# Moving zero writes, layer norms and hidden units in the first two layers of an eight-stage network kernel

## The chip, the cores and the metric

The kernel runs on one core of a Trainium2 chip. A core has TensorE (PE in the profile; PEld is its weight load), VectorE (DVE), ScalarE (ACT), GpSimd (POOL) and SyncE (SP, which here only issues DMAs). TensorE writes its results to PSUM, from where VectorE and ScalarE fetch them into SBUF. The metric is the device time of one execution in microseconds; lower is better.

## The reference

Sixteen blocks of 128 tokens with 256 channels (`x`, float32) go through four pairs of a cross attention and a feed-forward layer. Each of the eight layers begins with a layer norm of `x` over the channels and adds its output to `x`. The change is in the first pair:

```python
def _layernorm(x, axis=-1, eps=1e-05):
    m = jnp.mean(x, axis=axis, keepdims=True)
    v = jnp.var(x, axis=axis, keepdims=True)
    return (x - m) / jnp.sqrt(v + eps)

# first attention: 32 heads of 8 channels, keys and values from ctx (128 tokens a block)
q = apply_axial_rope((x @ Wq).reshape(b, n, 32, 8), pos)
k, v = jnp.split(ctx @ Wkv, 2, axis=-1)          # k gets the same rotation
w = softmax(einsum('bqhd,bkhd->bhqk', q, k) / sqrt(8))
out = einsum('bhqk,bkhd->bqhd', w, v).reshape(b, n, 256) @ Wout + bout

# product-key layer: 4 heads, two sets of 128 keys, 2048 hidden units, 8 of them chosen a head
sim1, sim2 = q1 @ keys[:, :, 0], q2 @ keys[:, :, 1]
s1, i1 = top_k(sim1, 8); s2, i2 = top_k(sim2, 8)
final_scores, pk_idx = top_k(s1[..., :, None] + s2[..., None, :], 8)
hidden = silu(x . e_down[chosen]) * relu(final_scores)
out = sum over chosen of hidden * e_up[chosen]

x = x + attention(_layernorm(x)); x = x + product_key(_layernorm(x)); ...
```

## The kernel before

One program holds all layers; `run` (from L1625 on) loads the packed weights of each layer into two alternating SBUF slots, "even" and "odd", and calls the layers in order. The program is traced through a layer that makes all semaphores and, for each engine, a fixed order of instructions: a planner goes through the traced instructions with a model of their costs and lets each engine take, whenever it is free in that model, the earliest traced instruction that is ready. On the chip every engine then runs its instructions strictly in that order. `tc.issue_after(ins)` puts what is traced inside it, as far as it is on the engine of `ins`, behind `ins`. `tc.high_priority()` lets a few matmuls go ahead. Tiles of one tag in a pool share the pool's buffers in turn.

**Start.** `setup` (L69 on) loads two blocks of `x`, small constants and makes the identity. `run` then loads the attention's weights, the other blocks of `x`, and the product-key layer's weights `w_f0` (5 MB) into the odd slot; it writes zeros into a tile `zero` (L1652) and sends it 14 times to a scratch in DRAM (for a later layer). `rope_tables` (L185 on) makes cosines and sines on VectorE and ScalarE from `pos`.

**A norm.** `ln` (L136 on) makes for each block two VectorE instructions, BATCH_NORM_STATS2 (L143) and BATCH_NORM_AGGREGATE (L144), then for the group two on GpSimd, an addition (L119) and a power (L120, `rsqrt_pool`), and then for each block one VectorE instruction, xn (L154). `lnT` transposes the result on TensorE (pxT, L168) and fetches it to xnT by ScalarE and VectorE in turn (L67, L65).

**First attention** (`l0_attn`). It first writes zeros into three tiles `vx` (values with zeros between the heads, 1280 columns each) and `own` (zeros with ones, for the sums of the softmax): these are GpSimd's MEMSETs of L234 and L235. `inputs(g)` makes a group's norms: group 0 is blocks 0 and 1, then four blocks a group. For one block, `front` makes queries, keys and values (pqk, pv; L251 to L267), `turn` the transposes and the block-diagonal keys `kbd` (L279, L282 on GpSimd), and `start(b, c)` a half of the heads: `l0_terms` makes the scores S on TensorE (L322, into a single PSUM buffer), and twice, for half of S, a maximum (L330), a subtraction into E (L331, the second one is kept as `l0_last`) and the exponential on ScalarE (L332). `l0_heads` transposes E (pT, L181), copies (eT, L344), multiplies with `vx` and `own` into po (L350), and divides (rz L361, oT L362). `l0_out` projects (py, L370) and adds to `x` (L371). The loop over blocks runs them interleaved: the second half of block b is started while the first half is finished, and `front` is two blocks ahead. In it, group b // 4 + 2 is traced at b = 3, 7, 11, ahead of everything else of that block, and group 1 before the loop, tied behind `l0_last`.

**Product-key layer** (`l0_ffn`). Its pools take over the SBUF and PSUM of the attention's. `normed(g)` makes the norm of two blocks. `scores(b)` makes the queries fq (L403) and, in `peer_scores`, their products with both sets of keys (fs, L462; sim, L466), maxima and thresholds on VectorE and GpSimd. `units(b, q)` makes a quarter of the 16 groups of hidden units (fh, L417) and their SiLU (sh, L421). `peer_table(b, half)` makes, for a half of the keys, a table of sums g of each of four heads (two heads on GpSimd, L501, two on ScalarE, L507) and keeps what is over the threshold (L511, VectorE). `peer_weights` transposes the tables into one sum (r, L525) and multiplies with the units (wT, L529). `peer_up` multiplies with the last matrix (fy, L538). Before the loop come norm, scores, table and four units of block 0, and two units of block 1 (`first`); in the loop each half makes the next table behind the current wT, and the next block's units two by two, if they were not made.

Of the kernel before, what the change touches and what calls it, by code (L numbers as in the profile page):

```python
# [8 lines left out]
F32 = mybir.dt.float32  # L9
# [6 lines left out]
ALU = mybir.AluOpType  # L16
# [4 lines left out]
P = 128  # L21
# [31 lines left out]
class Net:  # L53
# [50 lines left out]
        at, w = ROWS[name]  # L104
        return self.rows[:, at : at + w]

    def load(self, pool, name, tag, step=2048):

        src = self.a[name]
        n = src.shape[1]  # L110
        t = pool.tile([P, n], F32, tag=tag, name=f"w_{name}")
        for i, at in enumerate(range(0, n, step)):
            end = min(n, at + step)
            self.nc.sync.dma_start(out=t[:, at:end], in_=src[:, at:end])
        return t

    def rsqrt_pool(self, out, var, n):

        self.nc.gpsimd.tensor_tensor(out, var, self.eps5.to_broadcast([P, n]), ALU.add)  # L119
        self.nc.gpsimd.tensor_tensor(out, out, self.mhalf.to_broadcast([P, n]), ALU.pow)  # L120

    def rsqrt(self, pool, x, n, tag, key):

# [32 lines left out]
            )  # L156
        return xn

    def lnT(self, pool, psum, bs, ptag="tr", rsqrt=None, bufs=None):

        nc = self.nc
        xn = self.ln(pool, bs, rsqrt=rsqrt, bufs=bufs)
        n = len(bs)
        xT = pool.tile([P, 2, n * P], F32, tag="xnT", name=f"xnT{bs[0]}")
        for c in range(2):
            ps = psum.tile([P, 512], F32, tag=ptag, name=f"pxT{bs[0]}_{c}")
            for i in range(n):
                nc.tensor.transpose(  # L168
                    ps[:, i * P : (i + 1) * P], xn[:, i, c * P : (c + 1) * P], self.ident
                )  # L170
            self.evac(xT[:, c, :], ps[:, : n * P])
        return xn, xT
# [42 lines left out]
    def l0_attn(self, w):  # L215

        nc, tc = self.nc, self.tc
        Wq = w[:, 0:512].rearrange("p (c n) -> p c n", c=2)
        Wk = w[:, 512:768]
        Wv = w[:, 768:1024]  # L220
        Wo = w[:, 1024:1536].rearrange("p (c n) -> p c n", c=2)
        with ExitStack() as es:
            op = es.enter_context(tc.tile_pool(name="l0o", bufs=1))
            xp = es.enter_context(tc.tile_pool(name="l0x", bufs=2))
            sp = es.enter_context(tc.tile_pool(name="l0s", bufs=2))
            kp = es.enter_context(tc.tile_pool(name="l0k", bufs=3))
            tr = es.enter_context(tc.tile_pool(name="l0tr", bufs=3, space=PSUM))
            sc = es.enter_context(tc.tile_pool(name="l0sc", bufs=1, space=PSUM))
            pvp = es.enter_context(tc.tile_pool(name="l0pv", bufs=1, space=PSUM))

            own = op.tile([P, 160], F32, tag="own", name="own")
            vx = [op.tile([P, 8, 160], F32, tag=f"vx{k}", name=f"vx{k}") for k in range(3)]
            for t in (*vx, own):
                nc.gpsimd.memset(t, 0.0)  # L234
            nc.gpsimd.memset(own.rearrange("p (i k) -> p i k", k=40)[:, :, 0:8], 1.0)  # L235
            xTs, turned, ready, terms, outs, after = {}, {}, {}, {}, {}, {}

            def inputs(g):
                bs = [b for b in range(max(4 * g - 2, 0), 4 * g + 2) if b < self.nb]
                if bs:  # L240
                    xT = self.lnT(xp, tr, bs, rsqrt=self.rsqrt_pool)[1]
                    for i, b in enumerate(bs):
                        xTs[b] = xT[:, :, i * P : (i + 1) * P]

            def front(b):

                if b >= self.nb:
                    return
                xT = xTs.pop(b)
                pqk = tr.tile([P, 2, 256], F32, tag="tr", name=f"pqk{b}")  # L250
                nc.tensor.matmul(pqk[:, 1, :], self.ctxT[:, b, :], Wk, start=True, stop=True)  # L251
                for c in range(2):
                    nc.tensor.matmul(pqk[:, 0, :], xT[:, c, :], Wq[:, c, :], start=c == 0, stop=c == 1)
                pv = tr.tile([P, 32, 8], F32, tag="tr", name=f"pv{b}")
                nc.tensor.matmul(pv.rearrange("p h d -> p (h d)"), self.ctxT[:, b, :], Wv, start=True, stop=True)
                qk = sp.tile([P, 512], F32, tag="qk", name=f"qk{b}")
                t = sp.tile([P, 512], F32, tag="t", name=f"t{b}")
                by_head = lambda a: a.rearrange("p (h a two) -> p h a two", a=4, two=2)
                src = pqk.rearrange("p t (h a two) -> p (t h) a two", a=4, two=2)
                nc.vector.tensor_tensor(by_head(qk), src, bc(self.cosT[:, b], 1, 64), ALU.mult)  # L260
                for k in range(2):
                    nc.vector.tensor_tensor(
                        by_head(t)[:, :, :, k], src[:, :, :, 1 - k], bc(self.sinT[:, b, :, k], 1, 64), ALU.mult
                    )
                nc.gpsimd.tensor_tensor(qk, qk, t, ALU.add)
                v = vx[b % 3]
                nc.scalar.copy(  # L267
                    v.rearrange("p g (i k) -> p g i k", k=40)[:, :, :, 0:8], pv.rearrange("p (g i) d -> p g i d", i=4)
                )
                turned[b] = (qk, v)  # L270

            def turn(b):

                if b >= self.nb:
                    return
                qk, v = turned.pop(b)
                ps = self.transposes(tr, lambda i: qk[:, i * P : (i + 1) * P], 4, f"pqkT{b}")
                qkT = kp.tile([P, 4, P], F32, tag="qkT", name=f"qkT{b}")
                nc.scalar.copy(qkT, ps)  # L279
                kbd = kp.tile([P, 2, 4, P], F32, tag="kbd", name=f"kbd{b}")  # L280
                for c in range(2):
                    after[b] = nc.gpsimd.tensor_tensor(  # L282
                        kbd[:, c], bc(qkT[:, 2 + c, :], 1, 4), bc(self.mask8, 2, P), ALU.mult
                    )
                ready[b] = (qkT, kbd, v)

            def start(b, c):
                if b < self.nb:
                    terms[b, c] = self.l0_terms(sp, kp, sc, b, c, *ready[b][:2])

            inputs(0)
            front(0)
            front(1)
            turn(0)
            turn(1)
            start(0, 0)
            with tc.issue_after(self.l0_last.ins):
                inputs(1)
            for b in range(self.nb):
                if b % 4 == 3:  # L300
                    inputs(b // 4 + 2)
                start(b, 1)
                front(b + 2)
                outs[b] = sp.tile([P, 2, P], F32, tag="oT", name=f"oT{b}")
                self.l0_heads(sp, kp, tr, pvp, b, 0, terms.pop((b, 0)), ready[b][2], own, outs[b])
                if b:
                    self.l0_out(tr, b - 1, outs.pop(b - 1), Wo, after[min(b + 1, self.nb - 1)])
                start(b + 1, 0)
                self.l0_heads(sp, kp, tr, pvp, b, 1, terms.pop((b, 1)), ready.pop(b)[2], own, outs[b])
                turn(b + 2)  # L310
            b = self.nb - 1
            self.l0_out(tr, b, outs.pop(b), Wo, after[b])
# [61 lines left out]
    def l0_ffn(self, w):  # L374

        nc, tc = self.nc, self.tc
# [4 lines left out]
        with ExitStack() as es:  # L381
            xp = es.enter_context(tc.tile_pool(name="f0x", bufs=2))
# [3 lines left out]
            mm = es.enter_context(tc.tile_pool(name="f0mm", bufs=4, space=PSUM))  # L386
# [4 lines left out]
            def normed(g):  # L391
                if g * 2 < self.nb:
                    bs = list(range(2 * g, min(2 * g + 2, self.nb)))
                    _, xT = self.lnT(xp, mm, bs, ptag="mm", rsqrt=self.rsqrt_pool)
                    for i, b in enumerate(bs):
                        xTs[b] = xT[:, :, i * P : (i + 1) * P]

# [27 lines left out]
            chosen = scores(0)  # L425
            G = self.peer_table(gp, 0, 0, chosen)
            sh = [units(0, q) for q in range(4)]
            first = [units(1, q) for q in range(2)] if self.nb > 1 else []
            for b in range(self.nb):
                more = b + 1 < self.nb  # L430
                nxt, after = first, None
                first = []
# [1192 lines left out]
    def run(self):  # L1625

        tc = self.tc
# [7 lines left out]
        loaded = []  # L1635
        pools = [None, self.wpool]
        for i, (_, _, stages) in enumerate(plan):
            if i == 0:

                with tc.tile_pool(name="w0", bufs=1) as pool:  # L1640
                    loaded = [self.load(pool, *plan[0][:2], step=1024)]
                    load = lambda out, in_: self.nc.sync.dma_start(out=out, in_=in_)
# [3 lines left out]
                            load(self.rows, self.a["rows"][0:NALL].partition_broadcast(P))  # L1646
                        load(self.x[b], self.a["x"][b])
                    load(self.gains, self.a["gains"])
                    loaded.append(self.load(self.wpool, *plan[1][:2]))

                    zero = pool.tile([P, 8 * D], F32, tag="zero", name="zero")
                    self.nc.gpsimd.memset(zero, 0.0)  # L1652
# [161 lines left out]
```

## Time and profile before

| | |
|---|---|
| median of 3 runs | 2497.4 us (2489.95 to 2499.14) |
| profiled execution | 2492.25 us, its span 2490.5 us |
| mean granted TensorE clock | 0.974 |
| first attention, 0 to 281 us | PE busy 249.61, DVE 229.91, ACT 153.07, POOL 75.55 us |
| product-key layer, 281 to 695 us | PE 389.90, DVE 342.89, ACT 220.71, POOL 167.78 us |
| the other layers, 695 to 2490.5 us | PE 1642.30, DVE 1150.22, ACT 674.44, POOL 503.60 us |

A line of the timeline has the start of an instruction or of several alike in us, their time in us, the engine, the line in the kernel, the operation, the output and inputs by the program's names, the shapes and the count. In brackets is how long the engine had been idle and who ended that. Busy times are sums of the instructions' times; as matmuls overlap, a busy TensorE is not TensorE at its peak. The granted clock is a share of full speed.

### The profile page before, as it was taken

To read this page: it belongs to the slowest core of one execution; us is meant where nothing else is said; L and a number is where in the kernel's file an instruction comes from. 1 tells how busy PE (TensorE), PEld (TensorE's weight loads), DVE (VectorE), ACT (ScalarE), POOL (GpSimd) and SP (SyncE) were. 2 spreads that over 40 slices of the span, in tenths; PEclk is the share of its full clock that TensorE was granted. 3 is DMA by queue.
4 is the path that set the end of the run, shared out by engine and by line. 5 is a ranking of instruction groups with operands and counts; after the bars stand their busy time and mean duration, and the time that the engine had idled before them with its cause. 6 is when DMAs were issued, how large, how long until landed. Compare 5 with 4: busy or idle time off the path is not lost. (4 is left out here: it accounts for less than half of the span.)

```text
span 2490.5 us, 39604 instructions
## 1 busy us (share of the span) xinstructions
PE 2281.8 (92%) x14876; PEld 1709.7 (69%) x14876; DVE 1723.0 (69%) x3904; ACT 1048.2 (42%) x2778; POOL 746.9 (30%) x678
## 2 busy tenths in 40 slices
PE   6999799999989999998997778899899999999798
PEld 3666589898977777775884455555577777776465
DVE  6888788888865555565574999831466666668964
ACT  3656455455533443432331333411455555554121
POOL 3222234343411322222002433100222332224665
PEclk8999899999999999998999899999999999999999
DMA  9000200000030000002223000000100000000000
GB/s 376 17 2 2 86 1 1 1 1 1 1 121 2 19 10 10 10 13 84 69 71 137 25 14 10 1 0 1 69 1 1 1 1 1 1 1 1 7 13 15
DMA packets 29678, 74.57 MB, mean 30 GB/s; under 512 B 6688, under 2 KB 21160, under 8 KB 23856
## 3 DMA queue, kind: packets, MB, share of 16 engines
q1 hardware_dynamic: 25200, 62.06, 6.7%
q0 software_dynamic: 3072, 8.39, 1.0%
q8 instruction: 119, 1.95, 0.3%
q10 hardware_dynamic: 1216, 1.59, 0.2%
q14 instruction: 71, 0.58, 0.1%
HBM read 46.07 MB, written 25.95 MB: 29 GB/s over the span
## 5 line engine op out<-in xcount | busy, mean ns | idle before, releaser
L501 POOL TENSOR_TENSOR g<-sim 128x1024 f32<-128x1024 f32 x64 | 140.2, 2212 | 221.1 <-ACT sim L466 186.4
L181 PE MATMUL pT<-ident,E 128*128 128x128 f32 x1280 | 196.0, 283 | 9.8 <-POOL E L631 7.5
L511 DVE SCALAR_TENSOR_TENSOR g<-g,th 128x1024 f32<-128x1024 f32 x128 | 194.3, 1577 | 0.0
L181 PEld LDWEIGHTS pT<-ident,E 128*128 128x128 f32 x1280 | 147.0, 144 | 51.7 <-issue 21.8
L507 ACT ACTIVATE g<-sim 128x128 f32<-128x128 f32 x512 | 159.8, 390 | 32.0 <-PE r L525 31.5
L626 ACT ACTIVATE E<-E,mx 128x128 f32<-128x128 f32 x256 | 99.5, 390 | 160.1 <-DVE mx L623 138.7
L1464 POOL TENSOR_TENSOR E<-E,rs 128x512 f32<-128x512 f32 x64 | 66.6, 1041 | 302.0 <-DVE rs L1463 148.6
L1459 ACT ACTIVATE E<-S,mx,sc 128x128 f32<-128x128 f32 x256 | 113.9, 455 | 98.8 <-DVE mx L1455 89.6
L525 PE MATMUL r<-ident,g 128*128 128x128 f32 x1024 | 124.6, 277 | 19.9 <-DVE g L511 19.8
L525 PEld LDWEIGHTS r<-ident,g 128*128 128x128 f32 x1024 | 115.4, 142 | 27.7 <-DVE g L511 17.5
L661 PE MATMUL py<-w_w_l,oT 128*128 128x256 f32 x512 | 128.1, 383 | 5.2 <-DVE x L663 3.6
L1492 PE MATMUL py<-w_w_l,oT 128*128 128x256 f32 x512 | 131.1, 383 | 0.1
L1492 PEld LDWEIGHTS py<-w_w_l,oT 128*128 128x128 f32 x512 | 93.6, 190 | 46.9 <-issue 39.2
L631 POOL TENSOR_TENSOR E<-E,rs 128x512 f32<-128x512 f32 x64 | 66.7, 1042 | 193.5 <-DVE rs L630 119.8
L417 PE MATMUL fh<-xnT,w_w_f 128*128 128x128 f32 x1024 | 122.7, 279 | 0.0
L600 PE MATMUL pt<-xnT,w_w_l 128*128 128x256 f32 x512 | 121.1, 382 | 0.0
L661 PEld LDWEIGHTS py<-w_w_l,oT 128*128 128x128 f32 x512 | 93.9, 190 | 39.4 <-issue 20.1
L417 PEld LDWEIGHTS fh<-xnT,w_w_f 128*128 128x128 f32 x1024 | 118.6, 194 | 1.8
L538 PE MATMUL fy<-w_w_f,wT 128*128 128x256 f32 x512 | 118.4, 379 | 0.0
L1406 PE MATMUL pq<-xnT,w_w_l 128*128 128x256 f32 x512 | 116.2, 380 | 1.0 <-ACT xnT L67 0.6
L600 PEld LDWEIGHTS pt<-xnT,w_w_l 128*128 128x128 f32 x512 | 94.9, 192 | 15.2 <-issue 2.5
L1406 PEld LDWEIGHTS pq<-xnT,w_w_l 128*128 128x128 f32 x512 | 94.8, 190 | 14.4 <-ACT sqk L1372 1.2
(401 smaller groups left out, 5505.7 us busy)
## 6 DMA issues: line engine op xcount, KB each, us to landing
w_w_f<-in_w_f SPq DMA_DIRECT2D x14, 1024.0 KB, 11.2
sent<-zero SPq DMA_DIRECT2D x14, 1024.0 KB, 20.2
w_w_l<-in_w_l SPq DMA_DIRECT2D x14, 1024.0 KB, 11.1
xb<-sent SPq DMA_DIRECT2D x38, 128.0 KB, 2.0
back<-yb SPq DMA_DIRECT2D x38, 128.0 KB, 1.9
x<-in_x SPq DMA_DIRECT2D x16, 128.0 KB, 4.9
out<-x SPq DMA_DIRECT2D x16, 128.0 KB, 1.7
ctx<-in_ctx ACTq DMA_DIRECT2D x1, 1024.0 KB, 8.4
```

Source lines behind the costliest of these rows:

```text
L181: self.nc.tensor.transpose(ps[:, i, :], src(i), self.ident)
L417: nc.tensor.matmul(ps[:, k, :], down[:, c, a * P : (a + 1) * P], xT[:, c, :], start=c == 0, stop=c == 1)
L501: nc.gpsimd.tensor_tensor(g, bc(sim[:, 2 * h, 8 * half : 8 * half + 8], 2, P), bc(sim[:, 2 * h + 1, :], 1, 8), ALU.add)
L507: nc.scalar.activation(g[:, k, :], sim[:, 2 * h + 1, :], AF.Identity, bias=sim[:, 2 * h, a : a + 1])
L511: nc.vector.scalar_tensor_tensor(gf, gf, th[:, h : h + 1], gf, ALU.is_ge, ALU.mult)
L525: nc.tensor.matmul(ps[:, k, :], G[h][:, 4 * q + k, :], self.ident, start=h == 0, stop=h == 3, is_transpose=True)
L538: self.nc.tensor.matmul(py, wT[:, k, :], up[:, a, :], start=a == 0, stop=a == 15)
L600: nc.tensor.matmul(ps[:, k], A[:, h + k, c, :], xT[:, c, :], start=c == 0, stop=c == 1)
L661: nc.tensor.matmul(pys[b], oT[:, j, :], Wo[:, h, :], start=h == 0, stop=h == 15)
L1406: nc.tensor.matmul(ps[:, l], Wq[:, c, h * P : (h + 1) * P], xT[:, c, :], start=c == 0, stop=c == 1)
L1459: nc.scalar.activation(E[:, j, :], S[:, j, :], AF.Exp, bias=mx[:, j : j + 1], scale=sc[:, i, 0, r, j : j + 1], accum_out=rs[:, j : j + 1],)
L1492: nc.tensor.matmul(pys[b], oT[:, j, :], Wo[:, h, :], start=h == 0, stop=h == 15)
```

## The change

Four edits in the first two layers:

1. The zeros of `vx` and `own` are traced after `inputs(0)`, tied on GpSimd behind the power of that first norm (`self.root`).
2. In the attention's loop, `start(b, 1)` is traced first, and `inputs` of the later groups behind it, tied on VectorE behind the last subtraction of that `start`.
3. The product-key layer's norm of blocks 0 and 1 is made in the attention at b = 6, with the attention's pools, tied like the norms of edit 2. Its transposed result lies in 512 columns that are added to the tile of `w_f0` (`xT2`), and `normed(0)` takes it from there.
4. Before the loop of the product-key layer, four units of block 1 are traced instead of two. The loop then makes none for that block.

```diff
-    def load(self, pool, name, tag, step=2048):
+    def load(self, pool, name, tag, step=2048, more=0):
         src = self.a[name]
         n = src.shape[1]
-        t = pool.tile([P, n], F32, tag=tag, name=f"w_{name}")
+        t = pool.tile([P, n + more], F32, tag=tag, name=f"w_{name}")
...
-        self.nc.gpsimd.tensor_tensor(out, out, self.mhalf.to_broadcast([P, n]), ALU.pow)
+        self.root = self.nc.gpsimd.tensor_tensor(out, out, self.mhalf.to_broadcast([P, n]), ALU.pow)
...
-    def lnT(self, pool, psum, bs, ptag="tr", rsqrt=None, bufs=None):
+    def lnT(self, pool, psum, bs, ptag="tr", rsqrt=None, bufs=None, xT=None):
...
-        xT = pool.tile([P, 2, n * P], F32, tag="xnT", name=f"xnT{bs[0]}")
+        xT = pool.tile([P, 2, n * P], F32, tag="xnT", name=f"xnT{bs[0]}") if xT is None else xT[:, :, : n * P]
...
-            for t in (*vx, own):
-                nc.gpsimd.memset(t, 0.0)
-            nc.gpsimd.memset(own.rearrange("p (i k) -> p i k", k=40)[:, :, 0:8], 1.0)
...
             inputs(0)
+            with tc.issue_after(self.root.ins):
+                for t in (*vx, own):
+                    nc.gpsimd.memset(t, 0.0)
+                nc.gpsimd.memset(own.rearrange("p (i k) -> p i k", k=40)[:, :, 0:8], 1.0)
             front(0)
...
             for b in range(self.nb):
-                if b % 4 == 3:
-                    inputs(b // 4 + 2)
                 start(b, 1)
+                with tc.issue_after(self.l0_last.ins):
+                    if b % 4 == 3:
+                        inputs(b // 4 + 2)
+                    if b == min(6, self.nb - 1):
+
+                        bs = [k for k in range(2) if k < b]
+                        self.aheadT = bs, self.lnT(xp, tr, bs, rsqrt=self.rsqrt_pool, xT=self.xT2)[1]
                 front(b + 2)
...
-                    _, xT = self.lnT(xp, mm, bs, ptag="mm", rsqrt=self.rsqrt_pool)
+                    if bs == self.aheadT[0]:
+                        xT = self.aheadT[1]
+                    else:
+                        _, xT = self.lnT(xp, mm, bs, ptag="mm", rsqrt=self.rsqrt_pool)
...
-            first = [units(1, q) for q in range(2)] if self.nb > 1 else []
+            first = [units(1, q) for q in range(4)] if self.nb > 1 else []
...
-                    loaded.append(self.load(self.wpool, *plan[1][:2]))
+
+                    loaded.append(self.load(self.wpool, *plan[1][:2], more=512))
+                    self.xT2 = loaded[1][:, 10240:10752].rearrange("p (c n) -> p c n", c=2)
```

## The prediction

> **What bounds the kernel now.** I read the busy time by stages first, since the page's 92% for TensorE is a mean over seven very different layers. The change touches only 0 to about 340 us: the first attention (0 to 281 us) and the start of the product-key layer. The first fence is that table. After each stretch and its length come the busy times of PE, PEld, DVE, ACT and POOL (instructions in brackets), then the granted TensorE clock, the DMA share and GB/s.
>
> ```profile
> 20.00:30.00 10.00, 4.08 (x18) 1.87 (x17) 8.82 (x22) 4.09 (x5) 3.95 (x5) 0.65 1.00 383
> 30.00:40.00 10.00, 7.45 (x54) 4.94 (x52) 8.91 (x20) 3.90 (x8) 1.31 (x3) 0.84 1.02 428
> 40.00:50.00 10.00, 6.71 (x75) 4.44 (x73) 8.47 (x18) 4.91 (x9) 4.26 (x7) 0.84 1.01 422
> ...
> 200.00:240.00 40.00, 39.33 (x497) 25.19 (x491) 33.97 (x45) 23.62 (x37) 10.70 (x11) 1.00 0.01 2
> 280.00:320.00 40.00, 29.86 (x211) 27.16 (x212) 26.55 (x70) 18.34 (x49) 13.77 (x17) 0.83 0.33 132
> ```
>
> Three places leave TensorE idle: the first 10 us (it does 0.13 us of work), 20 to 50 us, where VectorE is 87% busy and TensorE 61% at a reduced clock, and 280 to 312 us. Between them the attention runs at 15.2 us a block: the POOL rows of kbd start at 69.33 and, 12 blocks later, at 252.00, and (252.00 - 69.33) / 12 = 15.2.
>
> The second view is the timeline of the start.
>
> ```profile
> 3.21 3.60 DVE L193 COPY ang<-pos 128x32 f32<-128x32 f32 x1 [3.21 <-DMA pos<-in_pos]
> 3.23 3.37 POOL L234 MEMSET vx<- 128x1280 f32 x3
> ...
> 3.39 3.44 DVE L143 BATCH_NORM_STATS2 st<-x 128x6 f32<-128x256 f32 x1
> ...
> 6.54 0.22 POOL L234 MEMSET own<- 128x160 f32 x1
> ...
> 8.56 0.76 POOL L120 TENSOR_TENSOR rs<-rs,mhalf 128x2 f32<-128x2 f32 x1
> ...
> 9.30 0.19 DVE L213 COPY sinT<-sFalse 128x64 f32<-128x64 f32 x1
> 9.40 0.73 DVE L154 TENSOR_SCALAR xn<-x,mv,rs 128x256 f32<-128x256 f32 x2
> ```
>
> A VectorE copy of 32 columns takes 3.60 us, where one of 64 takes 0.19: it ends at 6.81, just behind the last zero-writing (6.54 + 0.22 = 6.76). The copy is held while GpSimd writes zeros, and the first statistics wait behind it.
>
> The third view is the timeline from 29 us.
>
> ```profile
> 29.40 0.72 DVE L143 BATCH_NORM_STATS2 st<-x 128x6 f32<-128x256 f32 x2
> ...
> 31.99 1.38 DVE L154 TENSOR_SCALAR xn<-x,mv,rs 128x256 f32<-128x256 f32 x4 [1.09 <-POOL rs L120]
> ...
> 33.29 1.21 DVE L330 TENSOR_REDUCE mx<-S 128x8 f32<-128x1024 f32 x1
> ```
>
> The scores of block 0's second half were made by 24.75 + 2.09 = 26.84, yet their maximum starts at 33.29: statistics and norms of blocks that nobody needs yet stand in front of it.
>
> The fourth view is the passage between the layers.
>
> ```profile
> 280.13 0.70 PE L370 MATMUL py<-w_w_l,oT 128*128 128x256 f32 x2 [1.41 <-DVE oT L362]
> ...
> 285.63 3.76 PE L403 MATMUL fq<-xnT,w_w_f 128*128 128x128 f32 x16 [0.30 <-ACT xnT L67]
> ...
> 303.14 0.45 PE L525 MATMUL r<-ident,g 128*128 128x128 f32 x1 [4.52 <-DVE g L511]
> ...
> 305.99 5.51 PE L417 MATMUL fh<-xnT,w_w_f 128*128 128x128 f32 x32
> ...
> 311.34 3.00 PE L525 MATMUL r<-ident,g 128*128 128x128 f32 x26
> ```
>
> From the last projection (ends 280.83) to the first query matmul, 4.8 us pass with only the norm of blocks 0 and 1 in between, though those blocks were finished some 200 us earlier. Then fq takes 3.76 us at half clock; the same 16 matmuls take 1.95 at 314.18.
>
> **Zeros behind the first norm.** Without the hold, the first statistics end near 3.39 + 0.39 = 3.8 instead of 6.83: 3.05 us, and the path (statistics, POOL, xn, TensorE) has no other cover, so it counts in full. Against it stands the new place: the five zero-writings (3 x 1.12 + 0.22 + 0.12 = 3.7 us) start as pow ends, where VectorE's last table copies and xn run. Here a rule of the Trainium skill speaks against the change ("SBUF — State Buffer", section "Who interferes with whom"): GpSimd and a VectorE copy or tensor_scalar in a two-port mode exclude each other for a whole instruction, whichever comes first. By the rule with xn as such an instruction, xn would start near 6.2 + 3.7 = 9.9 instead of 9.40: 0.5 lost. The rows speak less strictly: xn takes 0.316 to 0.414 us in 32 instances, 256 columns at one a cycle of that page's 0.96 GHz (an estimate of 0.27), so it runs in no such mode; and the three table copies before 9.30 overlap pow unharmed. Only the last copy races with the first zero. I take 3.0 gained and keep -0.5. The zeros are needed by the copy into vx (13.80), 4 us later; POOL's next own work starts at 14.75.
>
> **Norms behind subtractions.** Statistics of blocks 6 to 15 leave the start: 10 x (0.31 + 0.08) = 3.9 us; and xn of blocks 6 to 13: 8 x 0.345 = 2.8. VectorE sets the pace there, so 6.7 us. They return at blocks 3, 7 and 11, behind the second subtraction of a half. VectorE's rows at 80 to 240 us show 16 waits of 16.3 us in all for S, about 1 us each; four statistics (1.56) nearly fit in one. The 2.8 of xn do not: they come one POOL round trip later (0.28 + 1.0), between a maximum and its subtraction, where VectorE paces S (one S buffer). What queues behind: VectorE's next maxima, POOL's kbd behind the rs instructions (needed a half-block later), TensorE's transposes. For TensorE waiting in order I add 0.5 a group, from its 1.57 at 28.40 and 0 when the norm was early: 1.5. Net 6.7 - 2.8 - 1.5 = 2.4. Ends: 6.7, if all falls into idle time; a loss of 16, if each of the three groups costs a half-round of 7.6 (3 x 7.6 - 6.7).
>
> **The product-key norm in the attention.** fq no longer waits for statistics, POOL, xn, four transposes and their evacuation. It can start when the last addition has freed its PSUM buffer (280.94 + 0.42 = 281.4): 4.2 us. The gap is then 0.6 us, so I cost fq at full clock, 1.95: 1.8 more. The chain behind it (sim, tables, r) is serial, so 6.0 count. Price at block 6: two statistics (0.78, in the S wait), two xn (0.73), one VectorE evacuation (0.36), and 0.5 for TensorE's order: 1.6. Its POOL pair finds POOL 27% busy (10.70 of 40 us). The transposes move. Net 4.4; ends 6.0 and, with a half-round lost, -1.6. The destination is columns behind the weights in a slot that the later w_f1 makes larger anyway: no DMA is added, the w_f load keeps its pieces of 1 MB, and SP's queue is unchanged.
>
> **More units first.** Two more units of block 1 (2 x 1.83 = 3.65 us of TensorE) come before r. If TensorE's order puts all four into its wait for g (298.6 to 306.7, 8.1 us), r ends near 306.7 + 3.5 = 310.2 instead of 314.3: 4 gained. But in the rows, six of r stand first, wait, and fh comes between them and the other 26; four units there delay r by 3.65, and VectorE (idle 6.4 before wT at 313.03) and the next tables follow. Of that some returns: r of block 1's second half starts at 350.97 though its last table was done at 348.33. The old order is the nearest row, so a loss of 3.65 - 2.64 = 1.0; ends +4 and -3.65.
>
> **The sum.** 3.0 + 2.4 + 4.4 - 1.0 = 8.8 us. The profiled run took 2492.25 (span 2490.5, 1.75 around it), and would take 2483.4. The median of the runs shown is 2497.4, 5.15 above it; I keep that distance: 2488.6.
>
> **Rivals.**
> - Everything pays: zeros 3.0, norms 5.5 (xn mostly in idle time), passage 5.5, units 4.0: 18.0, so 2479.4. For it: the idle is there in each place. Against: TensorE's order around r.
> - Work is only moved: VectorE is the pace-setter at the start and in the rounds, so the 6.7 come back in full, the copy loses its race (-0.5), the units cost 3.65, and 4.4 remain: 0.3, so 2497.1.
> - Slower: the tied norms cost whole half-rounds. Place: blocks 3, 6, 7 and 11, where TensorE's transposes, in fixed order, wait for xn tied behind a subtraction and hold S. Price up to 7.6 each, 30.4, against 3.0 + 6.7 + 6.0 - 3.65 = 12.1 of everything else: 18.3 slower, 2515.7. It decides from 3.0 us an insertion on (no gain), and is over 0.5% slower from 6.2 on. For it: one S buffer and TensorE over 98% occupied there. Against: VectorE's 1 us waits.
>
> **How the numbers follow.** Half a per cent, 12.5 us, is about what a measurement of this kernel can tell from no change. My sum 0.36 (own range 2482 to 2494), all pays 0.31 (2472 to 2486), moved 0.12 (2493 to 2503), slower 0.21 (2505 to 2522). Faster than 2484.9: 0.14 of the first, 0.30 of the second, 0.44. Slower than 2509.9: 0.19 of the last. Within: 0.37. The range 2475 to 2511 leaves out 0.04 below and about 0.15 above.
>
> **What would show it.** Right: the first BATCH_NORM_STATS2 near 0.4 us long and xn near 6.3; the second half's maximum within 3 us of S; fq within 1 us of the attention's last addition and near 2 us long. Wrong: xn near 10 us; waits of pxT for xn of several us at four places; a block time over 15.2 in those blocks; fh x64 between six and 26 of r, with wT later than before relative to sim; or a different block time in the product-key layer (now 26.1 us, kept by TensorE at 25.3), which this sum leaves unchanged.

## The result, and the profile after

The changed kernel takes 2505.09 us (median; 2502.74 to 2508.24), the kernel before 2493.92 us beside it on the same chip (2488.67 to 2499.14). The ratio is 1.0044, with a 95% interval of 1.0034 to 1.0054: 11 us slower. The profiled execution of the changed kernel has a span of 2503.3 us at a granted clock of 0.973 (before: 2490.5 at 0.974).

Three numbers locate it. The last addition to `x` in the attention starts 16.8 us later, at 297.72 instead of 280.94 us (the first row is the kernel before, the second the changed one):

```profile
280.94 0.42 DVE L371 TENSOR_TENSOR x<-py,x 128x256 f32<-128x256 f32 x1 [0.86 <-PE py L370]
297.72 0.42 DVE L377 TENSOR_TENSOR x<-py,x 128x256 f32<-128x256 f32 x1 [0.86 <-PE py L376]
```

The first addition of the product-key layer follows it by 53.34 us instead of 54.91: 1.6 back. From there to the end of the two spans another 2.4 come back. So the loss is in the attention, and it is larger than the whole. It is not at its start, as the same stretches as before show (times, then PE, PEld, DVE, ACT, POOL busy, clock, DMA share, GB/s; 70 to 90 us is added):

```profile
20.00:30.00 10.00, 5.11 (x19) 2.97 (x20) 8.25 (x18) 3.84 (x4) 3.18 (x4) 0.66 1.00 384
30.00:40.00 10.00, 9.76 (x108) 7.15 (x106) 7.40 (x10) 5.10 (x9) 1.27 (x1) 0.83 1.02 425
40.00:50.00 10.00, 8.76 (x114) 5.83 (x112) 8.33 (x11) 6.34 (x11) 2.73 (x3) 1.00 1.01 423
70.00:80.00 10.00, 6.22 (x102) 4.28 (x98) 9.44 (x11) 4.63 (x8) 2.89 (x4) 1.00 0.01 2
80.00:90.00 10.00, 6.28 (x21) 3.90 (x22) 8.23 (x17) 2.61 (x3) 1.22 (x2) 0.56 0.00 0
```

TensorE does more from 20 to 50 us than before (30 to 40 us: 9.76 for 7.45), but from 80 to 90 us it runs 21 matmuls at a granted clock of 0.56. The kernel before has these two rows there:

```profile
70.00:80.00 10.00, 9.93 (x117) 6.33 (x115) 8.46 (x11) 5.72 (x11) 3.29 (x4) 1.00 0.01 2
80.00:90.00 10.00, 9.93 (x127) 6.68 (x125) 10.00 (x15) 6.37 (x12) 2.73 (x3) 1.00 0.01 2
```

TensorE's row of the timeline of the changed kernel shows what it does meanwhile:

```profile
76.12 1.14 PE L328 MATMUL S<-kbd,qkT 32*128 32x512 f32 x8 [0.43 <-DVE E L337]
82.42 2.09 PE L328 MATMUL S<-kbd,qkT 32*128 32x512 f32 x8 [5.15 <-DVE E L337]
85.81 2.30 PE L168 MATMUL pxT<-ident,xn 128*128 128x128 f32 x8 [1.30 <-DVE xn L154]
...
91.31 1.43 PE L181 MATMUL pT<-ident,E 128*128 128x128 f32 x9
```

This is the round of block 3. The scores of its second half start at 76.12; for the scores of block 4's first half TensorE then waits 5.15 us, until the subtraction frees the one buffer of S, then 1.30 for xn, and only at 91.31 come the transposes pT of block 3's first half, whose exponential had ended at 77.16. The S at 82.42 takes 2.09 us where 1.14 is usual: the granted clock is one half there, as is shown below. VectorE's row of the same time shows the tied norm:

```profile
81.05 1.22 DVE L337 TENSOR_TENSOR E<-S,mx 128x1024 f32<-128x1024 f32 x1
82.19 0.74 DVE L143 BATCH_NORM_STATS2 st<-x 128x6 f32<-128x256 f32 x2
...
85.34 1.38 DVE L154 TENSOR_SCALAR xn<-x,mv,rs 128x256 f32<-128x256 f32 x4 [1.41 <-POOL rs L120]
86.64 1.22 DVE L336 TENSOR_REDUCE mx<-S 128x8 f32<-128x1024 f32 x1
```

The statistics start where the tie puts them, right behind the subtraction; xn starts 4.3 us after the subtraction does, and TensorE's order has put S and pxT ahead of pT. Summed over 74 to 280 us, the waits of TensorE (who waited for whom: us in total, times, longest) are in the changed kernel:

```profile
PE S L328 <- DVE E L337: 10.7, 4, 5.2
PE pxT L168 <- DVE xn L154: 6.9, 4, 3.3
```

and in the kernel before:

```profile
PE S L322 <- DVE E L331: 1.2, 1, 1.2
PE po L350 <- DVE oT L362: 0.9, 1, 0.9
```

Four waits for xn, where the kernel before shows none in this stretch: that is what the rival "slower" had named.

To see which rounds lose, I take the start of GpSimd's kbd: round b is the time from the kbd of block b + 1 to that of block b + 2. All kernels that follow are in this table too (us; "start" is the kbd of block 4, where round 3 begins; "end" is the last addition of the attention).

| kernel | start | round 3 | round 6 | round 7 | round 11 | end |
|---|---|---|---|---|---|---|
| before | 81.6 | 15.6 | 16.4 | 16.7 | 16.3 | 280.9 |
| changed | 73.9 | 30.2 | 20.9 | 21.5 | 18.6 | 297.7 |
| only the tie | 75.0 | 29.9 | 13.9 | 28.5 | 24.2 | 304.5 |
| changed, tied norms traced later | 73.5 | 22.4 | 20.9 | 21.3 | 20.8 | 290.7 |
| changed, own PSUM buffer | 82.5 | 23.3 | 17.6 | 22.8 | 18.5 | 311.2 |
| changed, without the tie | 81.7 | 16.7 | 16.6 | 15.6 | 16.3 | 281.6 |
| changed, transposes apart | 73.9 | 21.7 | 18.3 | 14.7 | 18.3 | 279.1 |
| the same, two units | 73.5 | 20.2 | 18.3 | 14.7 | 18.3 | 277.2 |
| without the tie, two units | 79.6 | 16.7 | 16.6 | 15.6 | 16.3 | 279.4 |
| only the zeros | 80.7 | 15.6 | 16.4 | 16.7 | 16.3 | 280.0 |
| without the tie, two units, zeros moved further | 80.5 | 16.7 | 16.6 | 15.6 | 16.3 | 280.4 |
| the same, only block 3's group tied | 74.8 | 20.2 | 15.6 | 15.4 | 16.3 | 281.3 |
| without the tie, two units, zeros by ScalarE | 77.8 | 16.7 | 16.6 | 15.6 | 16.3 | 277.3 |

In the changed kernel rounds 3, 6, 7 and 11, the ones with a tied norm, take 14.6 + 4.6 + 4.8 + 2.3 = 26.3 us more than before. The start gains 7.7. What is left between these two and the 16.8 lies in the other rounds and behind the last kbd.

Where do the 26.3 go? In these four rounds TensorE stands idle for 19.1 us in the changed kernel and for 1.3 in the kernel before: 17.8 more. The rest goes with the clock. The granted clock is below 1 in exactly these four of the rounds 2 to 13, and in none of them in the kernel before; these are the four stretches:

```profile
81.20:91.44 10.24, 7.72 (x25) 4.93 (x26) 7.80 (x18) 1.64 (x2) 1.22 (x2) 0.50 0.00 0
139.23:146.05 6.82, 6.06 (x19) 3.79 (x20) 4.76 (x11) 1.43 (x2) 0.90 (x2) 0.50 0.01 4
163.12:166.53 3.41, 3.22 (x12) 2.87 (x13) 2.53 (x6) 0.58 (x1) 0.00 (x0) 0.50 0.00 0
227.97:231.39 3.42, 3.12 (x10) 2.62 (x11) 3.07 (x5) 0.37 (x1) 0.00 (x0) 0.50 0.00 0
```

TensorE is busy for 20.1 us in them at a clock of 0.50. If that work had taken half the time at full clock, it cost about 10 us; this is an estimate from these rows. 17.8 and 10 are a little more than the 26.3, so by this estimate idle time and clock together account for the loss.

The start itself, on VectorE and GpSimd (changed kernel):

```profile
3.09 0.23 DVE L193 COPY ang<-pos 128x32 f32<-128x32 f32 x1 [3.09 <-DMA pos<-in_pos]
3.27 0.42 DVE L143 BATCH_NORM_STATS2 st<-x 128x6 f32<-128x256 f32 x1
...
5.92 1.25 DVE L212 TENSOR_SCALAR sinT<-sFalse 128x64 f32<-128x64 f32 x1
6.02 1.18 DVE L213 COPY sinT<-sFalse 128x64 f32<-128x64 f32 x1
6.12 2.46 DVE L154 TENSOR_SCALAR xn<-x,mv,rs 128x256 f32<-128x256 f32 x2
```

```profile
5.28 0.77 POOL L120 TENSOR_TENSOR rs<-rs,mhalf 128x2 f32<-128x2 f32 x1
5.94 3.75 POOL L291 MEMSET vx<- 128x1280 f32 x3
```

The first statistics are 0.42 us long, so the old hold is gone; but now the two xn are held, 2.46 us where they took 0.73. And the passage to the product-key layer, on TensorE:

```profile
298.19 2.05 PE L412 MATMUL fq<-w_w_f 128*128 128x128 f32 x16 [0.59 <-DVE x L377]
...
316.60 0.66 PE L534 MATMUL r<-ident,g 128*128 128x128 f32 x2 [7.13 <-DVE g L520]
317.86 0.66 PE L534 MATMUL r<-ident,g 128*128 128x128 f32 x2 [0.60 <-DVE g L520]
318.31 8.18 PE L426 MATMUL fh<-w_w_f 128*128 128x128 f32 x64
326.33 3.22 PE L534 MATMUL r<-ident,g 128*128 128x128 f32 x28
```

fq starts 0.5 us after the last addition and takes 2.05; all 64 matmuls of four units stand between the first four of r and the other 28.

### The profile page after: what moved, and what is told of

It is laid out like the page before. It is cut to its first block, busy times and chain, and to the rows that moved or that the text cites. A ratio compares the mean times of both kernels' runs of the same rounds, so it can differ in the third digit from the quotient of the medians.

```text
span 2503.3 us, 39579 instructions
## 1 busy us (share of the span) xinstructions
PE 2283.1 (91%) x14876; PEld 1712.3 (68%) x14876; DVE 1723.7 (69%) x3904; ACT 1047.0 (42%) x2778; POOL 747.0 (30%) x678
## 5 line engine op out<-in xcount | busy, mean ns | idle before, releaser
L181 PEld LDWEIGHTS pT<-ident,E 128*128 128x128 f32 x1280 | 148.0, 145 | 51.9 <-issue 21.7
L534 PEld LDWEIGHTS r<-ident,g 128*128 128x128 f32 x1024 | 113.5, 141 | 30.0 <-DVE g L520 16.4
L670 PEld LDWEIGHTS py<-w_w_l,oT 128*128 128x128 f32 x512 | 93.9, 190 | 39.4 <-issue 20.1
L426 PE MATMUL fh<-xnT,w_w_f 128*128 128x128 f32 x896 | 105.9, 276 | 0.0
L547 PEld LDWEIGHTS fy<-w_w_f,wT 128*128 128x128 f32 x512 | 93.7, 190 | 15.4 <-DVE wT L538 4.5
```

Source lines behind the costliest of these rows:

```text
L181: self.nc.tensor.transpose(ps[:, i, :], src(i), self.ident)
L426: nc.tensor.matmul(ps[:, k, :], down[:, c, a * P : (a + 1) * P], xT[:, c, :], start=c == 0, stop=c == 1)
L534: nc.tensor.matmul(ps[:, k, :], G[h][:, 4 * q + k, :], self.ident, start=h == 0, stop=h == 3, is_transpose=True)
L547: self.nc.tensor.matmul(py, wT[:, k, :], up[:, a, :], start=a == 0, stop=a == 15)
L670: nc.tensor.matmul(pys[b], oT[:, j, :], Wo[:, h, :], start=h == 0, stop=h == 15)
```

## The experiments

Theory A: the tie costs, because the transposes of a tied norm stand ahead of the heads' transposes in TensorE's fixed order; both take buffers of one tag ("tr"), which are handed out in the order in which the tiles are traced. Theory B: the loss comes from the other edits. Rival B': the tied norm's own round trip over VectorE and GpSimd is late, wherever its transposes stand.

### The tie alone, and the change without the tie

The kernel before with edit 2 alone:

```diff
-                if b % 4 == 3:
-                    inputs(b // 4 + 2)
                 start(b, 1)
+                with tc.issue_after(self.l0_last.ins):
+                    if b % 4 == 3:
+                        inputs(b // 4 + 2)
```

> The kernel before with only the second edit: start(b, 1) first, then the later groups' norms tied behind its last subtraction. Theory A (the tie stops TensorE: transposes of the norms stand ahead of the heads in its fixed order because they share PSUM buffers): the first three blocks gain about 8 us, blocks 3, 7 and 11 lose about 15, 5 and 2 and a few more between, so 12 to 16 us slower than before, about 2507 us. Theory B (the loss comes from the norm that was brought forward and from the four units, the tie is about neutral): within 4 us of before.

Measured: 2521.18 us, ratio 1.0102 (1.0085 to 1.0119). The tie alone loses about 25 us, more than I expected: round 7 now takes 28.5 us, nearly as long as round 3. TensorE's longest wait in total from 74 to 280 us:

```profile
PE S L323 <- DVE E L332: 15.5, 4, 5.2
```

The opposite, the changed kernel with edit 2 undone for both norms (zeros, product-key norm ahead and four units stay):

```diff
-                start(b, 1)
-                with tc.issue_after(self.l0_last.ins):
-                    if b % 4 == 3:
-                        inputs(b // 4 + 2)
-                    if b == min(6, self.nb - 1):
+                if b % 4 == 3:
+                    inputs(b // 4 + 2)
+                if b == min(6, self.nb - 1):
...
+                start(b, 1)
```

> The changed kernel without its second edit: norms traced first in the block as before and not tied (the product-key norm too). Both theories: the stops at blocks 3, 6, 7 and 11 go, and the first 50 us lose their 8 us again. Zeros gain about 1, the norm brought forward about 5, the four units cost about 4: 2 us less than before, near 2492 us. If it is at or above the changed kernel, the tie was not the cause.

Measured: 2492.37 us, ratio 0.9983 (0.9973 to 0.9992). The stops are gone, and with them the lead at the start. Theory B falls; the tie costs 1.0044 - 0.9983 = 0.6%, some 15 us, in the changed kernel. Why the tie alone costs 10 us more than in the changed kernel I can follow only in part. In the traces its attention ends 6.7 us later than the changed kernel's, and another 7.3 us lie behind the product-key layer, where all these kernels run the same instructions in the same order (see the last section).

### The tied norms traced behind the first half's heads

```diff
                 start(b, 1)
-                with tc.issue_after(self.l0_last.ins):
-                    ...
                 front(b + 2)
                 outs[b] = ...
+                last = self.l0_last
                 self.l0_heads(sp, kp, tr, pvp, b, 0, ...)
+                with tc.issue_after(last.ins):
+                    ...
```

> The changed kernel with one thing moved: the same tied norms are traced behind the heads of the block's first half instead of ahead of front. VectorE does the same work behind the same subtraction. Theory A: TensorE has the heads to do while statistics, power and xn run, so the stop goes; block 3 takes under 19 us (30.2 between two kbd in the changed kernel), blocks 6, 7 and 11 under 18, in all about 20 us less than the changed kernel, near 2485 us. Theory B' (VectorE's 3 us of added work and the round trip over GpSimd in the loop that sets the pace): no more than 4 us less than the changed kernel.

Measured: 2505.04 us, ratio 1.0041 (1.0027 to 1.0055): no gain that shows. Round 3 falls from 30.2 to 22.4, but 6, 7 and 11 stay at 21. The stop has moved to the next neighbour: pT of the first half now goes first, and pT of the second half stands behind pxT, which waits for the chain subtraction, statistics, power, xn:

```profile
83.17 1.14 PE L329 MATMUL S<-kbd,qkT 32*128 32x512 f32 x8 [0.52 <-DVE E L338]
87.67 0.66 PE L168 MATMUL pxT<-ident,xn 128*128 128x128 f32 x2 [3.35 <-DVE xn L154]
...
90.87 1.04 PE L181 MATMUL pT<-ident,E 128*128 128x128 f32 x8
```

The attention ends 7.0 us earlier than in the changed kernel, and the product-key layer's last addition comes 5.4 earlier, yet the span is the same 2503.3: the layers behind took 5.4 us longer here, at a granted clock of 0.971 instead of 0.973. The instructions there and their order are the same in both kernels. The last section shows how far this part differs from trace to trace; why stays open.

### An own PSUM buffer for the norms' transposes

```diff
-            tr = es.enter_context(tc.tile_pool(name="l0tr", bufs=3, space=PSUM))
+            tr = es.enter_context(tc.tile_pool(name="l0tr", bufs=2, space=PSUM))
+            nx = es.enter_context(tc.tile_pool(name="l0nx", bufs=1, space=PSUM))
...
-                    xT = self.lnT(xp, tr, bs, rsqrt=self.rsqrt_pool)[1]
+                    xT = self.lnT(xp, nx, bs, ptag="nx", rsqrt=self.rsqrt_pool)[1]
```

> The changed kernel with the norms traced where they are, but their transposes get one PSUM buffer of their own, taken from the three that all transposes and projections shared (two are left). Theory A: heads no longer queue behind the norms for a buffer, block 3 takes under 19 us between two kbd instead of 30.2, and the whole is 10 to 20 us less than the changed kernel, less what two buffers instead of three cost (up to 0.5 us a block). Theory B': block 3 stays near 30 us.

Measured: 2523.23 us, ratio 1.0108 (1.0091 to 1.0125). Round 3 falls to 23.3, but most other rounds take 16 to 19 us, also those without a norm. That two buffers are too few for the heads would explain it, but was not tested by itself. The run confounds two effects, and decides nothing about the total. It does show that pT may pass pxT once they share no buffers (it stands ahead of it here), and that 23.3 is still 8 more than before.

### The norm left where the change put it, its transposes apart

```diff
                 with tc.issue_after(self.l0_last.ins):
                     if b % 4 == 3:
-                        inputs(b // 4 + 2)
+                        xn = normed(b // 4 + 2)[1]      # statistics, power, xn
...
                 self.l0_heads(sp, kp, tr, pvp, b, 1, ...)
+                if b % 4 == 3:
+                    inputs(b // 4 + 2, xn)              # pxT and its copies
                 turn(b + 2)
```

and likewise for the product-key norm at b = 6.

> The changed kernel with the tied norm in two: statistics, root and normalised values stay where the change put them, behind the subtraction of (b,1), with the same VectorE and GpSimd work; the transposes into pxT and their copies are written behind the heads of (b,1), so that no transpose of a head stands behind them in the shared PSUM buffers. Theory A (TensorE stops because pxT stands in its fixed order ahead of the heads' transposes, in buffers that they share): the stops go, the interval between two filled kbd is below 18 us at blocks 3, 6, 7 and 11 (30.2, 20.9, 21.5 and 18.6 in the changed kernel), and the earlier start stays (third kbd near 74 us, 81.7 without the tie): 2485 to 2488. Rival B' (the tied norm's round trip over VectorE and GpSimd behind the subtraction is itself what is late, wherever the transposes stand): intervals stay above 20 us and the time within 3 us of 2505.

Measured: 2492.63 us, ratio 0.9987 (0.9977 to 0.9996). That takes 14 us off the changed kernel with the same work on VectorE and GpSimd, so most of the loss was TensorE's order: theory A. But its number, 2485 to 2488, is missed, and rounds 3, 6 and 11 are still 21.7, 18.3 and 18.3, over the 18 that I had named. The waits from 74 to 280 us show what is left:

```profile
PE po L363 <- DVE oT L375: 6.4, 5, 2.5
PE py L383 <- DVE oT L375: 1.4, 1, 1.4
```

S and pxT no longer wait to speak of; po waits for oT. VectorE's row in round 3 says why:

```profile
83.34 0.74 DVE L143 BATCH_NORM_STATS2 st<-x 128x6 f32<-128x256 f32 x2
...
84.86 0.92 DVE L374 RECIPROCAL rz<-po 128x128 f32<-128x128 f32 x1
...
87.24 1.38 DVE L154 TENSOR_SCALAR xn<-x,mv,rs 128x256 f32<-128x256 f32 x4 [1.11 <-POOL rs L120]
88.54 0.28 DVE L375 TENSOR_TENSOR oT<-po,rz 128x128 f32<-128x128 f32 x1
```

Statistics stand in front of rz, and xn, which itself waits for GpSimd's power, in front of oT. So B' fits the rest, by these rows: of round 3's surplus over the untied 16.7, 30.2 - 21.7 = 8.5 was TensorE's order and 21.7 - 16.7 = 5.0 is VectorE's. With that, the tie without its stop is worth nothing: the start's lead of 7.8 us over the untied kernel (73.9 for 81.7) is 2.5 at the end of the attention (279.1 for 281.6), and the ratios, 0.9987 and 0.9983, cannot be told apart. The granted clock from 20 to 60 us was 0.87 here and 0.83 there. Beside the untied kernel with two units of the next experiment, whose attention is the same and whose clock was 0.87 as well, the lead is 5.7 at the start and 0.3 at the end: 5.4 are given back in this pair, 5.3 in the other.

### Two units again, with and without the tie

`first = [units(1, q) for q in range(2)]` instead of `range(4)`, in the two kernels above.

> The same with two units written ahead of the first product-key block instead of four. If the units cost what the trace of the changed kernel shows between the similarity scores and the first weight (4.3 us, of which some 2 to 3 by POOL's later powers and not by the units): 1.5 to 3 us less than with four. If the units are free: no difference.

> Zeros behind the first norm and the product-key norm ahead, the other norms untied as before, two units. It leaves the two edits that should pay: zeros 1.2 and the product-key norm 5.9 less what POOL's powers take back (2.6): about 2488 to 2490 beside 2493.9 before; with the units at 1.5 to 3 us, 2492.4 without the tie minus that.

Measured: 2487.96 us, ratio 0.9970 (0.9957 to 0.9982), and 2486.31 us, ratio 0.9964 (0.9954 to 0.9974). Both are about 0.18% or 4.5 us below their partners with four units, more than the 1.5 to 3 expected. The trace gives 3.0 of it: from the attention's last addition to the first of the product-key layer it takes 53.65 us with four and 50.66 with two in the untied pair. In the other pair it is 53.36 and 50.97, so 2.4; what is left to 4.5 lies within the intervals. The rows of the untied kernel with two units (with four, fh takes 8.46 us there):

```profile
299.56 0.66 PE L533 MATMUL r<-ident,g 128*128 128x128 f32 x2 [0.60 <-DVE g L519]
300.01 5.49 PE L425 MATMUL fh<-w_w_f 128*128 128x128 f32 x32
305.34 3.22 PE L533 MATMUL r<-ident,g 128*128 128x128 f32 x28
```

8.46 - 5.49 = 2.97: the units stand inside r, at full price, and at the layer's last addition 2.5 of it are still there (2.1 in the other pair). Beside 54.91 in the kernel before, 50.66 also gives what the product-key norm ahead is worth by itself: 4.25 us.

### The zeros alone

The kernel before with edit 1 alone.

> Only the zeros behind the first root. By the prediction's step: 3.0 us less. By the trace of the changed kernel (the two normalised values took 2.46 us each while the memsets ran, the first score ended 1.2 us earlier): 1.2 us less, 2492.7. By the rival that the start is not on the path in the untied order: no difference.

Measured: 2494.74 us, ratio 0.9991 (0.9981 to 1.0000), between 0 and 4.7 us gained. The time cannot tell 3.0 from 1.2; the trace can: the first scores start at 17.36 instead of 18.52, 1.2 earlier as in the changed kernel (17.34), and the attention ends 1.0 earlier. (The 2.46 us named above are those of both normalised values together.)

### The zeros moved further, and one group tied

I wanted the zeros behind xn, in the untied kernel with two units:

```diff
-            with tc.issue_after(self.root.ins):
+            with tc.issue_after(self.norm.ins):      # the last xn of inputs(0)
```

> The kernel with zeros, product-key norm ahead and two units (2486.31, the other norms untied), but with the zeros written behind the first two normalised values instead of behind the first root. In the kernel with the zeros behind the root these two took 2.46 us (6.19 to 8.65), with a sine product and a copy held beside them (1.25 and 1.18). If the zeros hold them: 0.7 to 0.8 us for the two, no table operation over 0.3 us, xn done near 6.9 and the first score 1.5 to 1.8 us earlier, the time 1 to 2 us less (ratio near 0.9957 where it was 0.9964). If the two are slow for another reason: still 2.4 us, no difference.

Measured: 2486.14 us, ratio 0.9958 (0.9944 to 0.9972). The edit did not do what I meant: xn is VectorE's, and a tie orders only what is on the same engine, so the zeros became free, and GpSimd wrote the first between its addition and its power. It says nothing for or against moving them, but it shows the hold once more: two table instructions (the first at 5.16 takes 1.15 us; usually 0.18) end with the first zero-writing, and the two xn take 2.63 us.

In addition, only block 3's norm tied, with its transposes apart:

> The same, and in addition the norm of blocks 6 to 9 alone is tied behind the subtraction of block 3, with its transposes written behind block 3's heads; the others are untied. If the time that the ties gain at the start (third kbd near 74 us where the untied order has 79.6) is lost again in block 3 because statistics, root and values stand in front of the heads' products on VectorE there (21.7 and 20.2 us for block 3 with split transposes, 16.7 untied): attention ends within 2 us of the untied order and the time within 0.1%. If what the split order lost came from the other tied norms: 3 to 5 us less, near 2481.

Measured: 2487.22 us, ratio 0.9964 (0.9950 to 0.9978). The start leads by 5.7 us (74.8; 80.5 in the kernel just above), rounds 3 and 4 take 3.5 and 3.7 more (20.2 and 19.7 for 16.7 and 16.0), and the attention ends at 281.3, not earlier than that kernel's 280.4. The lead at the start is given back within two rounds, though only one norm was tied and its transposes stood behind the heads of its block.

### The zeros written by ScalarE

```diff
+            nc.scalar.copy(vx[0].rearrange("p h k -> p (h k)"), self.zero[:, 0:1280])
             with tc.issue_after(self.root.ins):
-                for t in (*vx, own):
-                    nc.gpsimd.memset(t, 0.0)
+                for t in vx[1:]:
+                    nc.scalar.copy(t.rearrange("p h k -> p (h k)"), self.zero[:, 0:1280])
+                nc.scalar.copy(own, self.zero[:, 0:160])
...
+                    self.zero = zero
```

> The kernel with zeros, product-key norm ahead, untied norms and two units, but the zeros of the three tiles are written by ScalarE, as copies from a tile of zeros that GpSimd has already made, and GpSimd writes only the 128x32 ones. If GpSimd's zero-writing is what holds VectorE (xn 2.46 us for two beside it, sine product 1.25): the two xn take 0.7 to 0.8 us, no operation of the tables over 0.3 us, the first score ends 1.3 to 1.7 us earlier than 18.55. If VectorE was slow there for another reason: xn still about 2.4 us. The time, if the start counts in full: ratio about 0.0006 below that of the zeros behind the root (0.9964).

Measured: 2482.94 us, ratio 0.9953 (0.9939 to 0.9966), the lowest of all. On VectorE:

```profile
5.82 0.19 DVE L212 TENSOR_SCALAR sinT<-sFalse 128x64 f32<-128x64 f32 x1
5.92 0.19 DVE L213 COPY sinT<-sFalse 128x64 f32<-128x64 f32 x1
6.02 0.73 DVE L154 TENSOR_SCALAR xn<-x,mv,rs 128x256 f32<-128x256 f32 x2
```

The hold is gone, so GpSimd's writing was it. The first scores start at 15.99, where 17.41 stood with the zeros on GpSimd (17.3 to 18.0 in seven traces with the zeros behind the power). The step in the ratio, 0.0011, is within the two intervals; what the traces show is at least 1.3 us at the first score.

## Why the prediction was wrong

The forecast was 2488.6 us, 8.8 less than before; it became 11 more. The measured time lies inside the range, but at the lower edge of what the rival "slower" was given (2505 to 2522, with 2515.7 as its sum), and the main forecast went the wrong way. Half a per cent was also too coarse as the limit of what can be told: the interval here is 0.1% to either side.

| step | forecast, us | measured, us |
|---|---|---|
| zeros behind the first norm | -3.0 | -1.2 (first scores) |
| norms off the start | -6.7 | -6.5 (kbd of block 4, less the zeros) |
| norms back at four places | +2.8 + 1.5 + part of 1.6 | +26.3 (rounds 3, 6, 7, 11) |
| product-key norm, passage | -6.0 | -5.9 at sim, -3.3 at the first table, -4.25 at the layer's first addition |
| two more units | +1.0 | +3.0 and +2.4 in two pairs (2.5 and 2.1 at the layer's last addition) |

**The step that failed** is "For TensorE waiting in order I add 0.5 a group, from its 1.57 at 28.40 and 0 when the norm was early: 1.5." The same 0.5 stands in the price of the product-key norm. So TensorE's waiting was put at 2.0 for four places, and the four rounds lost 26.3. The two rows averaged there were no neighbours of the new place. At 28.40 the attention was just starting, with TensorE 61% busy; the early norm had no wait at all. In the steady rounds TensorE is over 98% busy, and what stood behind pxT in its order was pT of the half that had long been ready; the prediction did not ask that. Its rival put the danger at the right four places, with the right mechanism (a fixed order, a tied xn, one S buffer) and nearly the right price: 30.4 in all for 26.3 measured, though spread unevenly, since round 3 alone lost 14.6 where 7.6 was the most for one place. In the sum the step stood at 1.5, and this rival got a chance of 0.21. No term was there for the clock, which made about 10 of the 26.3 by the estimate above; and rounds 4 and 5 took 2.1 us more as well. The weight against this rival, VectorE's waits of 1 us for S, was an argument about VectorE; the stop was TensorE's.

**Norms off the start** was right in size, and the wrong question. 6.7 forecast, 6.5 found; but the experiments with the transposes apart and with a single tied group show the lead given back in the next rounds even when TensorE no longer stops: 5.3 to 5.4 us with all groups tied, where the sum had 2.8. By the rows of round 3 the same statistics and xn then stand in front of rz and oT. The rival "work is only moved" had this part right.

**Zeros.** The old hold went as forecast: xn starts 3.3 us earlier. But the second xn ends only about 1.5 us earlier, and the first scores start 1.2 earlier. I set aside the rule of the Trainium skill ("SBUF — State Buffer", "Who interferes with whom") because I took xn's time for that of one column a cycle, and so for a sign that it runs in no two-port mode. The trace agrees with the rule's consequence: the two xn took 2.46 us beside the zeros and 0.73 with these on ScalarE. The second one started at 7.25 and ended at 8.58, just behind the second zero-writing (7.06 to 8.44). In which mode xn runs no run here shows. The upper bound (a start at 9.9) did not come, since xn gets in between two zero-writings: its first result was used at 7.39.

**Product-key norm** was right: fq 0.5 us behind the last addition and 2.05 us long, 5.9 us at sim for 6.0. Not foreseen was that GpSimd's additions and powers for the later blocks' norms, which used to be done before sim came, now end last in front of the tables:

```profile
305.27 0.70 POOL L120 TENSOR_TENSOR rs<-rs,mhalf 128x2 f32<-128x2 f32 x1
305.93 3.75 POOL L510 TENSOR_TENSOR g<-sim 128x1024 f32<-128x1024 f32 x2
```

sim was there at 303.23; 2.7 us pass, where the kernel before started the first table 0.1 us after sim. In all ten kernels with this norm ahead the first table starts 8.2 us behind the attention's last addition, whether the first sim was there after 5.0 us or after 7.0. The gain behind an early sim ended at the next queue.

**Units.** The order was as feared, 64 matmuls of fh inside r. The return of 2.64 us at a later r, which I had set against the 3.65, did not come: of the 3.0 us at the layer's first addition 2.5 are still there at its last, and 2.1 of the 2.4 in the other pair.

## What to carry to other kernels

In an order fixed ahead, price a moved step by what is queued behind it on each engine and which buffers that queue shares with it, not by the wait of the same step elsewhere: one late producer cost nearly a whole round here (14.6 us on 15.6). Ask too what an idle stretch does to TensorE's clock afterwards. Before moving work away from a stage where an engine sets the pace, see whether the place it goes to has idle time on that same engine ahead of the next product; here it had not, and undoing just the move showed it at once. When a hold between two engines is to go, try giving the work to an engine that isn't part of it, rather than to another time.

## What the runs showed of the hardware

- VectorE's xn, 256 columns with two scalars per row (four in 1.38 us when nothing holds it), was held by GpSimd's zero-writing: 2.46 us for two, 0.73 when ScalarE writes the zeros. Table instructions of 64 columns were held too (1.25 for 0.19). GpSimd's three writings took 3.75 us there, 3.37 in the kernel before. ScalarE's own copies of 1280 columns took 1.24 to 1.26 us, and the tables and xn beside them kept their usual times.
- Stops of TensorE came with a lower clock. In rounds 3, 6, 7 and 11 of the changed kernel the granted clock was 0.83, 0.84, 0.92 and 0.91, in its other rounds from 2 on, and in all of them in the kernel before and without the tie, 1.00. In round 3 TensorE went idle at 77.26, the clock fell to 0.50 at 81.20, and eight S matmuls took 2.09 us for 1.14. Where the limit lies is not shown: with a wait of 2.5 us in round 3 the clock of the round was 0.92 with all transposes apart and 1.00 with only block 3's group tied.
- Two kernels with the same attention, with four and with two units behind it, differed by 2.1 us at its end (281.55 and 279.41), and the clock from 20 to 60 us was 0.83 in one and 0.87 in the other. Differences of 2 us between two traces there are no finding.
- Behind the product-key layer all thirteen kernels run the same instructions in the same order on each engine, and that part took from 1778.6 us (changed) to 1787.4 us (only the zeros) in their traces, at granted clocks of 0.973 and 0.970. So the span of one trace cannot tell a gain of a few us in the first layers.
